# Experts' last biases gathered per slot, and a table of token ids in place of an array of dispatched rows

## The chip, the cores and the metric

The kernel runs on one core of a Trainium2 chip. The metric is the device time of one execution in microseconds (us). The engines are named as in the profile: PE (TensorE, the matmuls), PEld (PE's weight loads), DVE (VectorE), ACT (ScalarE), POOL (GpSimd) and SP (SyncE, which here issues most DMAs).

## The reference, cut to what matters

Two transformer layers run over x of 8 x 256 x 512, that is 2048 tokens of width C = 512, all in fp32. In the first layer attention and a mixture of experts read the same normalized tokens, and both results are added to x. The change touches the last biases of that mixture, b3 and sb3 below, and the way in which tokens get to their experts.

```python
xn = layernorm(x)
x  = x + lightning_attention(xn) + experts(xn)   # 32 heads of 128, decays, silu, RMS norm, gate
# experts: 16 of width 128, each token goes to 2 of them with a gate
for e in range(16):
    h = silu(xn @ w1[e] + b1[e]) * (xn @ w2[e] + b2[e])
    y = y + gate[:, e, None] * (h @ w3[e] + b3[e])
z = silu(xn @ sw1 + sb1) * (xn @ sw2 + sb2) @ sw3 + sb3   # shared expert of width 256, every token
experts = y + z
xn = layernorm(x)
x  = x + attention(xn) + low_rank_experts(xn)    # second layer
```

## The kernel before

The tokens stand in NCH = 4 chunks of CH = 512, each of TPC = 4 tiles of P = 128 tokens. The work is laid out in four stages.

**The opening** (until 164 us of the profiled execution) goes over the chunks. For each, `begin` normalizes on DVE; `turn_rows` (L243) turns the tokens on PE into xT, with copies by DVE; xns goes to DRAM as xnd; `token_sums` makes sums of the turned tokens on POOL and stores them (xc); `shared_up` (L312) runs the shared expert's first two products; `route` (L271 on PE, then a chain on DVE that ends in `first_two` and the gates `ge`) selects the two experts of each token; `decays` makes attention's decay factors on ACT and stores them (dec); `clear` has SP write zeros to a quarter of xd. Then `share` handles the chunk before: `shared_down` turns the gates (L333), copies them (ACT, L335), multiplies them by the 17 rows of last biases (16 experts' and the shared one, tile `b3_t`, L338), adds the shared expert's last products into the same PSUM bank (L340), and DVE adds the bank to x. The sum is stored as xr (L349). So the gate-weighted sum of the experts' last biases is made here, by a matmul over 17 rows with a column of ones for the shared bias.

After the last chunk DVE works out the slots (L475 to L523). Each expert's tokens are padded to whole tiles of 128, which makes NMT = 47 tiles and NSLOT = 6016 slots. `slots` has the slot of each token and choice, `slot_gates` its gate, `rows_` the rows of the expert's weights for each tile.

**The first pass of attention** (to 760 us; pass i = 0, on chunk 0) has NG = 8 units of 4 heads (g = 0 to 7). Products are made in seven parts p1 to p7 (`product`, L666), from sums of token blocks and sums of weights; the latter are made here by DVE and POOL and stored (ws) for the passes to come. Beside it `row` loads tiles of xnd (L1089), and `scatter` (L1094) writes their rows by an indirect DMA of POOL into xd, the array of dispatched rows, 2 x 16 times.

**Passes 1 to 3** (to 2510 us) have 24 units of some 75 us. Into them the 47 expert tiles are spread. A planner, `later(n, f)`, puts a piece of work n of its steps ahead, and `slot()` takes the pieces that are due. One `Expert` is four pieces: the start loads its rows xe from xd (SP, L696) and gathers its weights by `rows_` (POOL, L697), both into one buffer of `staged` (2 buffers, also used for weight blocks and for x); `turn`, 8 steps later, transposes the rows on PE; `up`, after 11, has the two products and their gating (L716); `down`, after 14, has the last product (L728), a copy by ACT to `ye` (L733) and the store to yd. `gather` and `settle` at the end of the passes read yd back by token, and multiply by the gates. At the end of each pass `load_sum` (L937) loads the chunk's xr on SP, and `finish` (L592) adds attention's sums to it on DVE; the result is stored as xs_. For the last chunk `next_x` (L1295) does the same in the tail.

**The tail** (to 2854 us) is the second layer. Its low-rank experts' products stand at L1434 and L1512.

The planner's order is kept as written on ACT and POOL (`manual_schedule`); on DVE, PE and SP the scheduler orders the instructions. Most tiles are rotated by name: tag "sum" has 3 buffers (ye, the loaded rows, others), `cp` 5. The helper `tt` at L97 issues all element-wise operations of two operands, so that many groups of the profile have that line; their tiles tell them apart. `Parts` cuts one large tile (`disp`, tag "acc", which attention later uses for its accumulators) into small ones, and `work` is the pool of the opening, whose memory attention takes over when it closes.

Of the kernel before, what the change touches and what calls it, by code (L numbers as in the profile page):

```python
# [18 lines left out]
P = 128  # L19
# [47 lines left out]
def block_kernel(  # L67
# [74 lines left out]

    def once(shape, name):
        return work.tile(shape, FP, tag=name, name=name, bufs=1)
# [19 lines left out]
    nc.sync.dma_start(out=bsh_t, in_=b_sh)  # L164
    b3_t = held[0 : E + 1, SH * C : (SH + 1) * C]
    nc.sync.dma_start(out=b3_t, in_=b3)
    for i in range(1, NCH):
# [6 lines left out]
    dram = ctx.enter_context(tc.tile_pool(name="dram", bufs=1, space=bass.MemoryType.DRAM))  # L174
    xd = dram.tile([NSLOT, C], FP, name="xd")
    yd = dram.tile([NSLOT, C], FP, name="yd")
# [5 lines left out]
    ]  # L182
    xnd = [dram.tile([P, TPC, C], FP, name=f"xnd{i}") for i in range(NCH)]
    dec = [dram.tile([P, 2, S + P], FP, name=f"dec{n}") for n in range(H // 2)]
# [3 lines left out]
    xr = [dram.tile([P, TPC, C], FP, name=f"xr{i}") for i in range(NCH)]  # L188
    zero = held[:, (SH + 1) * C : (SH + 2) * C].unsqueeze(1)
    nc.gpsimd.memset(zero, 0.0)  # L190

# [8 lines left out]

    before = once([P, E, E], "before")
    nc.gpsimd.memset(before, 1.0)
# [6 lines left out]

    dist = const.tile([P, S + P], FP, name="dist")  # L210
    nc.gpsimd.iota(
# [53 lines left out]
    def route(xT, ge, sel):  # L265

        full = [P, TPC, E]
        pl = ps_sc()
        for t in range(TPC):
            for c in range(NC):  # L270
                mm(  # L271
                    pl[:, bass.ts(t, E)], xT[:, c, bass.ts(t, P)], rw[:, c, :],
                    start=(c == 0), stop=(c == NC - 1),
                )
# [31 lines left out]
        tt(ge[:, :, 0:E], sc, sel, ALU.mult)  # L306
        nc.vector.memset(ge[:, :, E : E + 1], 1.0)

# [20 lines left out]
    def shared_down(i, hT):  # L329
        xc = xs[i]  # L330
        pg = ps_sc()
        for t in range(TPC):
            nc.tensor.transpose(pg[0 : E + 1, bass.ts(t, P)], gates[i][:, t, :], ident)  # L333
        gT = work.tile([E + 1, CH], FP, tag="geT", name="geT", bufs=1)
        nc.scalar.copy(gT, pg[0 : E + 1, :])  # L335
        for t in range(TPC):
            py = ps_mm()
            mm(py, gT[:, bass.ts(t, P)], b3_t, start=True, stop=False)  # L338
            for e in range(SH):
                mm(py, hT[:, e, bass.ts(t, P)], w3sh[:, e, :], start=False, stop=(e == SH - 1))  # L340
            tt(xc[:, t, :], py, xc[:, t, :], ALU.add)


    xT, gates, xns = [], [], []
    sel_all = once([P, NTT, E], "sel_all")

    def share(i, hT):
        shared_down(i, hT)
        nc.sync.dma_start(out=xr[i], in_=xs[i])  # L349

# [58 lines left out]

    def clear(i):  # L410
        lo, hi = (0, 12, 24, 36, NMT)[i : i + 2]
        nc.sync.dma_start(
            out=xd[lo * P : hi * P, :].rearrange("(j p) c -> p j c", p=P),
            in_=zero.to_broadcast([P, hi - lo, C]),
        )

    def begin(i):
# [5 lines left out]
    for i in range(NCH):  # L423
        xT.append(work.tile([P, NC, CH], FP, tag="xT", name=f"xT{i}", bufs=3))
        for t in range(TPC):
            turn_rows(xT[i], xns[i], t, ps_mm())
        nc.sync.dma_start(out=xnd[i], in_=xns[i])
        if i + 1 < NCH:
# [7 lines left out]
        ups.append(shared_up(i))  # L436
        ge = once([P, TPC, E + 1], f"ge{i}")
        route(xT[i], ge, sel_all[:, bass.ts(i, TPC), :])
        gates.append(ge)
        decays(i)  # L440
        clear(i)
        if i > 0:
# [6 lines left out]
    rows_ = const.tile([P, NMT], I32, name="rows_")  # L449
    disp = Parts(accp.tile([P, 7 * CH], FP, tag="acc", name="disp"))  # L450

# [48 lines left out]
    own = disp.tile([P, NMT], FP, name="own")  # L500
    nc.vector.tensor_reduce(own, owner, AX.X, ALU.add)
    nc.vector.tensor_scalar(own, own, float(E - 1), float(P), ALU.min, ALU.mult)
    nc.vector.tensor_scalar(rows_, own, part, None, ALU.add)
# [13 lines left out]
    for n in range(TOP):  # L517
        tt(hit, slot, ends_[:, n, :].unsqueeze(2).to_broadcast(full), ALU.is_equal)
        tt(hit, hit, sel_all, ALU.mult)
        for i in range(NCH):  # L520
            at_i = bass.ts(i, TPC)
            tt(hit[:, at_i, :], hit[:, at_i, :], gates[i][:, :, 0:E], ALU.mult)
        nc.vector.tensor_reduce(slot_gates[:, n, :], hit, AX.X, ALU.add)  # L523
# [62 lines left out]
    def finish(i, r):  # L586

        for b in range(2):
            for t in range(2):
# [3 lines left out]
                    o, acc[i][:, 2 * b : 2 * b + 2, t], all_rms[i][:, n : n + 1], o, ALU.mult, ALU.add  # L593
                )

    def spare8():
        return staged("spare")[:, 0 : TPC * C].rearrange("p (t c) -> p t c", t=TPC)

    with tc.tile_pool(name="attn", bufs=1) as attn, tc.manual_schedule(engines={mybir.EngineType.Activation, mybir.EngineType.Pool}):
# [79 lines left out]
        def slot():  # L679
# [3 lines left out]
            while pieces and pieces[0][0] <= now[0] and n < (2 if len(pieces) > 12 else 1):  # L683
                f = pieces.pop(0)[2]
                f()
                n += getattr(f, "func", f).__name__ not in ("silu", "gate", "row", "scatter", "load_sum", "sums1", "sums2", "sums3", "sums4", "settle0", "settle1", "out_sum")


        class Expert:


            def __init__(self, j):
                self.j = j
                xw = staged("xw")
                self.xe, self.we = xw[:, 0:C], xw[:, C:]
                nc.sync.dma_start(out=self.xe, in_=xd[bass.ts(j, P), :])  # L696
                nc.gpsimd.indirect_dma_start(  # L697
# [5 lines left out]
            def turn(self):  # L703
# [3 lines left out]
                self.xeT = attn.tile([P, NC, P], FP, tag="cp", name="xeT", bufs=5)  # L707
                nc.vector.tensor_copy(self.xeT, pt.rearrange("p (c n) -> p c n", c=NC))

            def up(self):  # L710
# [15 lines left out]
            def down(self):  # L726
# [5 lines left out]
                ye = attn.tile([P, C], FP, tag="sum", name="ye", bufs=3)  # L732
                nc.scalar.copy(ye, py)  # L733
                nc.sync.dma_start(out=yd[bass.ts(self.j, P), :], in_=ye)
# [75 lines left out]
        class Unit:  # L810
# [122 lines left out]
            def load_sum(self):  # L933

                if self.i + 1 < NCH:
                    self.r = spare8()
                    nc.sync.dma_start(out=self.r, in_=xr[self.i])  # L937

            def done(self):
# [140 lines left out]
        def expert(j):  # L1080
            e = Expert(j)
            later(8, e.turn)
            later(11, e.up)
            later(14, e.down)

        def row(t):

            x_ = attn.tile([P, C], FP, tag="sum", name="row", bufs=3)
            nc.sync.dma_start(out=x_, in_=xnd[t // TPC][:, t % TPC, :])  # L1089
            for n in range(TOP):  # L1090
                later(6 + 10 * n, partial(scatter, x_, t, n))

        def scatter(x_, t, n):
            nc.gpsimd.indirect_dma_start(  # L1094
                out=xd[:, :],
                out_offset=bass.IndirectOffsetOnAxis(ap=slots[:, n, t : t + 1], axis=0),
                in_=x_, in_offset=None, bounds_check=NSLOT - 1, oob_is_err=False,
            )

# [77 lines left out]
        for n, (i, g, p) in enumerate(plan):  # L1177
# [6 lines left out]
            if k == 0:  # L1184
# [104 lines left out]
    def next_x(i):  # L1289
# [332 lines left out]
```

## Time and profile before

| What | Value |
|---|---|
| runs before | 2852.0, 2856.99 and 2861.1 us, median 2856.99 |
| profiled execution | 2856.16 us, its span 2854.4 us |
| mean granted clock of TensorE | 0.993 |
| instructions | 49572 |
| moved in the span | 596 MB read from HBM, 163 MB written, 266 GB/s |

The durations below come from the one profiled execution. Its span is what the trace covers, and 1.8 us of its own time lie around that. In rows of the timeline stand start, length, engine, line, operation, output and inputs, shapes, type and count; the bracket gives the idle time of the engine ahead of the row, and what ended it. In rows of groups stand count, then busy time and mean ns of one, then the idle time ahead and its causes. In rows of DMA issues stand the queue, the kind, the count, and the median us from issue to landing.

### The profile page before, as it was taken

How to read it: one execution, taken by the hardware profiler on the slowest of the kernel's cores; microseconds unless marked ns; L12 is line 12 of the kernel's file. 1: busy time of each engine (PE TensorE's matmuls, PEld its weight loads, DVE VectorE, ACT ScalarE, POOL GpSimd, SP SyncE). 2: the span in 40 equal slices, each digit the busy share in tenths (PEclk: the TensorE clock that was granted, in tenths of full speed). 3: DMA queues.
4: the chain of work that ended last, by engine and by line, in shares of the span. 5: the costliest groups of instructions: out<-in, count | busy, mean ns of one | idle time of the engine just before them, and what ended most of it. 6: DMA issues, size and time to landing. Idle time of an engine off the chain costs nothing. (4 is left out here: it accounts for less than half of the span.)

```text
span 2854.4 us, 49572 instructions
## 1 busy us (share of the span) xinstructions
PE 2796.7 (98%) x19864; PEld 2566.1 (90%) x19864; DVE 1569.7 (55%) x2615; ACT 948.2 (33%) x1683; POOL 1465.7 (51%) x1213
## 2 busy tenths in 40 slices
PE   8989999999999999999999999999999999999999
PEld 4469999999999999999999999999999999987877
DVE  6555666666654445444545555555555555556663
ACT  3312222212244333333443333443444333432221
POOL 4545666665546555555645454545544566552210
PEclk9999999999999999999999999999999999999999
DMA  7888998899986777778877777777777788652211
GB/s 255 301 309 337 357 352 341 341 349 347 364 320 246 262 266 273 282 270 299 296 265 257 264 266 265 259 274 280 284 259 259 267 310 298 222 212 88 76 61 61
DMA packets 161943, 763.21 MB, mean 267 GB/s; under 512 B 18209, under 2 KB 24225, under 8 KB 109874
## 3 DMA queue, kind: packets, MB, share of 16 engines
q1 hardware_dynamic: 149826, 706.25, 66.9%
q0 software_dynamic: 11888, 53.79, 5.2%
q8 instruction: 157, 2.57, 0.4%
q14 instruction: 72, 0.59, 0.1%
HBM read 596.14 MB, written 163.05 MB: 266 GB/s over the span
## 5 line engine op out<-in xcount | busy, mean ns | idle before, releaser
L666 PE MATMUL ps_a<-xt,w 128*128 128x128 f32 x5376 | 750.9, 276 | 11.7 <-DVE r L97 7.7
L666 PEld LDWEIGHTS ps_a<-xt,w 128*128 128x128 f32 x5376 | 681.9, 192 | 30.1 <-issue 14.3
L97 POOL TENSOR_TENSOR c<-c 128x512 f32<-128x512 f32 x216 | 271.7, 1273 | 262.0 <-DVE c L97 259.9
L97 POOL TENSOR_TENSOR c<-c,r 128x512 f32<-128x512 f32 x240 | 318.4, 1347 | 158.9 <-DVE r L97 153.1
L666 PE MATMUL ps_e<-xt,w 128*128 128x128 f32 x2688 | 373.4, 275 | 1.3 <-DVE c L97 1.3
L97 POOL TENSOR_TENSOR sums<-sums,sq 128x512 f32<-128x512 f32 x120 | 153.3, 1278 | 426.4 <-ACT sq L796 425.6
L996 ACT COPY cp<-ps_a 128x512 f32<-128x512 f32 x336 | 196.4, 585 | 476.0 <-PE ps_a L666 468.8
L666 PEld LDWEIGHTS ps_e<-xt,w 128*128 128x128 f32 x2688 | 344.4, 192 | 11.2 <-issue 3.8
L97 POOL TENSOR_TENSOR w<-w 128x512 f32<-128x512 f32 x224 | 294.6, 1325 | 108.2 <-issue 31.2
L666 PE MATMUL ps_a<-w,xt 128*128 128x128 f32 x1792 | 346.7, 275 | 0.0
L858 PE MATMUL ps_sc<-wo,gT 128*128 128x256 f32 x1288 | 305.1, 379 | 1.8 <-POOL gT L97 1.8
L97 DVE TENSOR_TENSOR acc<-ps_sc,acc 128x512 f32<-128x512 f32 x208 | 143.3, 690 | 265.8 <-PE ps_sc L858 198.8
L666 PEld LDWEIGHTS ps_a<-w,xt 128*128 128x128 f32 x1792 | 272.3, 192 | 0.0
L97 DVE TENSOR_TENSOR c<-ps_a,c 128x512 f32<-128x512 f32 x232 | 157.9, 686 | 202.7 <-PE ps_a L666 201.7
L858 PEld LDWEIGHTS ps_sc<-wo,gT 128*128 128x128 f32 x1288 | 232.3, 190 | 26.8 <-POOL gT L97 2.0
L666 PE MATMUL ps_b<-xt,w 128*128 128x128 f32 x1680 | 236.4, 277 | 6.8 <-ACT c L1010 4.2
L801 DVE SCALAR_TENSOR_TENSOR gT<-ps_o,nw,c 128x256 f32<-128x256 f32 x256 | 112.0, 479 | 231.0 <-ACT sq L796 222.0
L666 PEld LDWEIGHTS ps_b<-xt,w 128*128 128x128 f32 x1680 | 217.3, 194 | 17.5 <-issue 8.2
L744 ACT ACTIVATE c<-c 128x512 f32<-128x512 f32 x256 | 148.9, 627 | 170.1 <-DVE c L97 170.0
L796 ACT ACTIVATE sq<-ps_o 128x512 f32<-128x512 f32 x120 | 71.6, 597 | 382.3 <-PE ps_o L782 382.3
L666 PE MATMUL ps_e<-w,xt 128*128 128x128 f32 x896 | 173.2, 275 | 0.0
L97 DVE TENSOR_TENSOR s<-ps_sc,decay 128x384 f32<-128x384 f32 x256 | 139.8, 552 | 40.7 <-PE ps_sc L770 38.1
(299 smaller groups left out, 4635.8 us busy)
## 6 DMA issues: line engine op xcount, KB each, us to landing
w<-in_w_att_dram SPq DMA_DIRECT2D x128, 1024.0 KB
st<-in_w_att_dram SPq DMA_DIRECT2D x32, 1024.0 KB
wo<-in_w_out_dram SPq DMA_DIRECT2D x113, 256.0 KB
decay<-dec SPq DMA_DIRECT2D x64, 384.0 KB
w<-ws0p SPq DMA_DIRECT2D x12, 1792.0 KB
w<-ws1p SPq DMA_DIRECT2D x12, 1792.0 KB
w<-ws2p SPq DMA_DIRECT2D x12, 1792.0 KB
w<-ws3p SPq DMA_DIRECT2D x12, 1792.0 KB
```

Source lines behind the costliest of these rows:

```text
L97: (eng or nc.vector).tensor_tensor(o, a, b, op)
L666: mm(bank[:, bass.ts(ty, P)], a, b, start=(first and ty == 0), stop=True, skip_group_check=True,)
L744: nc.scalar.activation(qk, qk, AF.Silu)
L796: nc.scalar.activation(sq, po, AF.Square)
L801: nc.vector.scalar_tensor_tensor(gT[:, h, :].rearrange("p (t n) -> p t n", t=2), po[:, bass.ts(h, S)].rearrange("p (t n) -> p t n", t=2), ...
L858: mm(py[:, bass.ts(t, S)], self.O[p][:, hh, bass.ts(t, P)], self.wo[p][:, hh, :], start=(t == 0 and hh == 0), stop=(hh == 1), skip_group_c ...
L996: nc.scalar.copy(c, bank)
```

## The change

The gate-weighted bias matmuls of the opening go away. Each expert tile gathers its last bias once per slot: a DMA of POOL reads row `own_[j]` of b3 into all 128 rows of xe, after the rows of tokens in xe have been turned, and DVE adds it as it moves the last product out of PSUM. The shared expert's last bias is loaded as a row to 128 partitions, and POOL adds it to xr where attention's sums are added (`last_bias`).

The array xd, its clears, the row loads and the scatters of rows go away too. A `table` in DRAM, one int32 per slot, is zeroed once; token ids are scattered into it in the first pass of attention (32 indirect DMAs of POOL, 4 bytes a row). The last unit of that pass reads the table and turns it (`whose`), and each expert gathers its rows from xnd by it, on POOL's queue instead of SP's. An empty slot has token 0. Besides, `before`, `sel_all`, `ge` and the slot arithmetic share the tile `disp`, `dist` is in the opening's pool, the stores of xr keep the order of the program, and the steps of an expert's pieces are 10, 12, 13 and 18 instead of 8, 11 and 14.

```diff
+    disp = Parts(accp.tile([P, 7 * CH], FP, tag="acc", name="disp"))
...
-    b3_t = held[0 : E + 1, SH * C : (SH + 1) * C]
-    nc.sync.dma_start(out=b3_t, in_=b3)
...
-    xd = dram.tile([NSLOT, C], FP, name="xd")
+    table = dram.tile([NSLOT, 1], I32, name="table")
...
-    zero = held[:, (SH + 1) * C : (SH + 2) * C].unsqueeze(1)
-    nc.gpsimd.memset(zero, 0.0)
+    none = once([NMT, P], "none", I32)
+    nc.gpsimd.memset(none, 0)
+    nc.sync.dma_start(out=table.rearrange("(j p) o -> j (p o)", p=P), in_=none)
...
-    before = once([P, E, E], "before")
+    before = disp.tile([P, E, E], FP, name="before")
...
-    dist = const.tile([P, S + P], FP, name="dist")
+    dist = once([P, S + P], "dist")
...
     def shared_down(i, hT):
         xc = xs[i]
-        pg = ps_sc()
-        for t in range(TPC):
-            nc.tensor.transpose(pg[0 : E + 1, bass.ts(t, P)], gates[i][:, t, :], ident)
-        gT = work.tile([E + 1, CH], FP, tag="geT", name="geT", bufs=1)
-        nc.scalar.copy(gT, pg[0 : E + 1, :])
         for t in range(TPC):
             py = ps_mm()
-            mm(py, gT[:, bass.ts(t, P)], b3_t, start=True, stop=False)
             for e in range(SH):
-                mm(py, hT[:, e, bass.ts(t, P)], w3sh[:, e, :], start=False, stop=(e == SH - 1))
+                mm(py, hT[:, e, bass.ts(t, P)], w3sh[:, e, :], start=(e == 0), stop=(e == SH - 1))
             tt(xc[:, t, :], py, xc[:, t, :], ALU.add)
...
-    sel_all = once([P, NTT, E], "sel_all")
+    sel_all = disp.tile([P, NTT, E], FP, name="sel_all")
 
     def share(i, hT):
         shared_down(i, hT)
-        nc.sync.dma_start(out=xr[i], in_=xs[i])
+        tc.keep_in_program_order(nc.sync.dma_start(out=xr[i], in_=xs[i]))
...
-        ge = once([P, TPC, E + 1], f"ge{i}")
+        ge = disp.tile([P, TPC, E], FP, name=f"ge{i}")
...
-        clear(i)
...
+    token = const.tile([P, NTT], I32, name="token")
+    nc.gpsimd.iota(token, pattern=[[P, NTT]], base=0, channel_multiplier=1)
...
+    def last_bias(r, t3):
+        nc.sync.dma_start(out=t3, in_=b3[E : E + 1].to_broadcast([P, C]))
+        for t in range(TPC):
+            add(r[:, t, :], r[:, t, :], t3, nc.gpsimd)
...
                 xw = staged("xw")
                 self.xe, self.we = xw[:, 0:C], xw[:, C:]
-                nc.sync.dma_start(out=self.xe, in_=xd[bass.ts(j, P), :])
+                nc.gpsimd.indirect_dma_start(
+                    out=self.xe, out_offset=None, in_=xnd[:, :],
+                    in_offset=bass.IndirectOffsetOnAxis(ap=whose[:, j : j + 1], axis=0),
+                    bounds_check=NT - 1, oob_is_err=False,
+                )
...
+            def bias(self):
+                nc.gpsimd.indirect_dma_start(
+                    out=self.xe, out_offset=None, in_=b3[:, :],
+                    in_offset=bass.IndirectOffsetOnAxis(ap=own_[:, self.j : self.j + 1], axis=0),
+                    bounds_check=E, oob_is_err=False,
+                )
...
                 ye = attn.tile([P, C], FP, tag="sum", name="ye", bufs=3)
-                nc.scalar.copy(ye, py)
+                add(ye, py, self.xe)
...
                     nc.sync.dma_start(out=self.r, in_=xr[self.i])
+                    last_bias(self.r, attn.tile([P, C], FP, tag="sum", name="sb3", bufs=3))
...
-            later(8, e.turn)
-            later(11, e.up)
-            later(14, e.down)
-
-        def row(t):
-            x_ = attn.tile([P, C], FP, tag="sum", name="row", bufs=3)
-            nc.sync.dma_start(out=x_, in_=xnd[t // TPC][:, t % TPC, :])
-            for n in range(TOP):
-                later(6 + 10 * n, partial(scatter, x_, t, n))
-
-        def scatter(x_, t, n):
+            later(10, e.turn)
+            later(12, e.bias)
+            later(13, e.up)
+            later(18, e.down)
+
+        def scatter(t, n):
             nc.gpsimd.indirect_dma_start(
-                out=xd[:, :],
+                out=table[:, :],
                 out_offset=bass.IndirectOffsetOnAxis(ap=slots[:, n, t : t + 1], axis=0),
-                in_=x_, in_offset=None, bounds_check=NSLOT - 1, oob_is_err=False,
+                in_=token[:, t : t + 1], in_offset=None, bounds_check=NSLOT - 1, oob_is_err=False,
             )
+
+        def read_table():
+            rows = attn.tile([P, P], I32, tag="h1", name="rows")
+            nc.sync.dma_start(out=rows[0:NMT], in_=table.rearrange("(j p) o -> j (p o)", p=P))
+            byno = attn.tile([P, P], FP, tag="he", name="byno")
+            def turn_table():
+                nc.vector.tensor_copy(byno[0:NMT], rows[0:NMT])
+                pt = ps_sc()
+                nc.tensor.transpose(pt[:, 0:NMT], byno[0:NMT, :], ident[0:NMT, 0:NMT])
+                nc.vector.tensor_copy(whose, pt[:, 0:NMT])
+            later(16, turn_table)
...
                 if i == 0:
-                    for e in range(2):
-                        later(1 + 24 * e, partial(row, 2 * g + e))
+                    for e in range(5 * g, min(5 * g + 5, TOP * NTT)):
+                        later(5 + 10 * (e - 5 * g), partial(scatter, e // TOP, e % TOP))
+                    if g == NG - 1:
+                        later(4, read_table)
...
             nc.sync.dma_start(out=x_, in_=xr[i])
+            last_bias(x_, work.tile([P, C], FP, tag="sb3", name="sb3", bufs=1))
             finish(i, x_)
```

More of the change, by code (lines that the diff above doesn't have):

```diff
@@ L141, in block_kernel, with once @@
     work = opening.enter_context(tc.tile_pool(name="work1", bufs=2))
-    def once(shape, name):
-        return work.tile(shape, FP, tag=name, name=name, bufs=1)
+    def once(shape, name, dtype=FP):
+        return work.tile(shape, dtype, tag=name, name=name, bufs=1)
+    disp = Parts(accp.tile([P, 7 * CH], FP, tag="acc", name="disp"))
     scratch = big("scratch").rearrange("p (h b) n -> p h (b n)", h=4)
@@ L182, in block_kernel @@
     ]
-    xnd = [dram.tile([P, TPC, C], FP, name=f"xnd{i}") for i in range(NCH)]
+    xnd = dram.tile([NT, C], FP, name="xnd")
     dec = [dram.tile([P, 2, S + P], FP, name=f"dec{n}") for n in range(H // 2)]
@@ L305, in route @@
         first_two(sel, masked, E)
-        tt(ge[:, :, 0:E], sc, sel, ALU.mult)
-        nc.vector.memset(ge[:, :, E : E + 1], 1.0)
+        tt(ge, sc, sel, ALU.mult)
     def project(pm, wi, block, i):
@@ L408, in token_sums @@
             nc.sync.dma_start(out=xc[i][:, ORDER.index(p), 4:8], in_=t)
[L410 to L415, printed above, removed]
     def begin(i):
@@ L426, in block_kernel @@
             turn_rows(xT[i], xns[i], t, ps_mm())
-        nc.sync.dma_start(out=xnd[i], in_=xns[i])
+        nc.sync.dma_start(
+            out=xnd[i * CH : (i + 1) * CH, :].rearrange("(t p) c -> p t c", p=P), in_=xns[i]
+        )
         if i + 1 < NCH:
@@ L449, in block_kernel @@
     rows_ = const.tile([P, NMT], I32, name="rows_")
-    disp = Parts(accp.tile([P, 7 * CH], FP, tag="acc", name="disp"))
+    own_ = const.tile([P, NMT], I32, name="own_")
+    whose = const.tile([P, NMT], I32, name="whose")
+    token = const.tile([P, NTT], I32, name="token")
+    nc.gpsimd.iota(token, pattern=[[P, NTT]], base=0, channel_multiplier=1)
     earlier = disp.tile([P, P], FP, name="earlier")
@@ L501, in block_kernel @@
     nc.vector.tensor_reduce(own, owner, AX.X, ALU.add)
+    nc.vector.tensor_scalar(own_, own, float(E - 1), None, ALU.min)
     nc.vector.tensor_scalar(own, own, float(E - 1), float(P), ALU.min, ALU.mult)
@@ L521, in block_kernel @@
             at_i = bass.ts(i, TPC)
-            tt(hit[:, at_i, :], hit[:, at_i, :], gates[i][:, :, 0:E], ALU.mult)
+            tt(hit[:, at_i, :], hit[:, at_i, :], gates[i], ALU.mult)
         nc.vector.tensor_reduce(slot_gates[:, n, :], hit, AX.X, ALU.add)
@@ L685, in slot @@
                 f()
-                n += getattr(f, "func", f).__name__ not in ("silu", "gate", "row", "scatter", "load_sum", "sums1", "sums2", "sums3", "sums4", "settle0", "settle1", "out_sum")
+                n += getattr(f, "func", f).__name__ not in ("silu", "bias", "gate", "read_table", "scatter", "load_sum", "sums1", "sums2", "sums3", "sums4", "settle0", "settle1", "out_sum")
         class Expert:
@@ L708, in turn @@
                 nc.vector.tensor_copy(self.xeT, pt.rearrange("p (c n) -> p c n", c=NC))
+            def bias(self):
[3 more added lines that the diff above has]
+                    bounds_check=E, oob_is_err=False,
+                )
             def up(self):
```

## The prediction

> **What bounds the kernel.** I read the page's first part, then the windows cut at the stages, then TensorE's (PE's) timeline of the opening, then what other engines and DMA queues show wherever the change touches them. In the windows the columns are: stretch, its length, busy time of PE, of its weight loads, of VectorE (DVE), ScalarE (ACT) and GpSimd (POOL), granted clock, DMA share, GB/s.
>
> ```profile
> PE 2796.7 (98%) x19864; PEld 2566.1 (90%) x19864; DVE 1569.7 (55%) x2615; ACT 948.2 (33%) x1683; POOL 1465.7 (51%) x1213
> ```
> ```profile
> 0.00:58.50 58.50, 47.29 (x152) 29.10 (x153) 40.21 (x88) 22.81 (x31) 27.98 (x45) 0.94 0.74 267
> 58.50:164.40 105.90, 96.93 (x288) 44.50 (x286) 56.11 (x113) 30.28 (x48) 53.96 (x84) 0.94 0.76 285
> 164.40:200.00 35.60, 27.39 (x217) 26.51 (x216) 24.02 (x55) 6.84 (x11) 7.24 (x6) 0.95 0.85 313
> 200.00:760.00 560.00, 555.34 (x4296) 535.92 (x4295) 347.04 (x533) 121.75 (x210) 343.81 (x269) 1.00 0.91 347
> 760.00:2240.00 1480.00, 1472.69 (x11235) 1400.70 (x11234) 744.48 (x1136) 584.83 (x1049) 781.79 (x616) 1.00 0.75 274
> ```
>
> PE is the bound from 200 us on: it idles 4.7 us in the first pass of attention (200 to 760) and 7.3 us in the 1480 us in which the experts run. There, work taken from DVE, ACT, POOL or the DMA queues can win at most those few us; work added to them can lose much more, if it makes PE wait. Only matmuls removed, and waits removed in the opening, buy time.
>
> **The opening, what goes.** Four times, once a chunk, the old code turns the gates (L333), copies them (ACT, L335) and adds bias products (L338) ahead of the shared expert's own products (L340). The last two chunks on PE (start, length, what; in brackets the idle time before):
>
> ```profile
> 131.91 1.12 PE L338 MATMUL ps_b<-held,geT 17*128 17x512 f32 x2 [0.67 <-ACT geT L335]
> 132.96 1.98 PE L340 MATMUL ps_b<-held,scratch 128*128 128x512 f32 x4
> ...
> 147.41 0.61 PE L333 MATMUL ps_sc<-ident,ge 128*17 128x128 f32 x4 [3.58 <-DVE ge L97]
> ...
> 149.58 2.07 PE L338 MATMUL ps_b<-held,geT 17*128 17x512 f32 x2
> 151.58 3.78 PE L340 MATMUL ps_b<-held,scratch 128*128 128x512 f32 x4
> 155.29 1.27 PE L338 MATMUL ps_a<-held,geT 17*128 17x512 f32 x2
> ```
>
> One bias product takes 1.05 us from start to start (131.91 to 132.96). Twelve at 1.05 are 12.6 us; the last chunk's four are 2.00, 1.20, 1.05 and 1.05, so 5.3. The turn and the wait for its copy take 1.26 us in each of three chunks (130.65 to 131.91), 3.8. In the last chunk the turn (0.45) waits 3.58 for the router's gates; afterwards PE runs slow, and L340 takes 3.71 instead of 1.92 (1.8). In all 12.6 + 5.3 + 3.8 + 0.45 + 3.58 + 1.8 = 27.5 us.
>
> **What of it is given back.** After the shared expert PE turns the next chunk, and that needs PSUM banks and the copies (xT) that DVE makes among its routing work:
>
> ```profile
> 75.16 0.66 PE L243 MATMUL ps_a<-ident,xn 128*128 128x128 f32 x4 [1.32 <-DVE x L97]
> 76.97 3.48 PE L271 MATMUL ps_sc<-rw,xT 128*128 128x16 f32 x16 [1.15 <-DVE xT L248]
> ```
>
> PE would come 5.5 us earlier (4 x 1.05 + 1.26) to this point, but DVE is solid here from 63.7 to 76.8. It gains only what leaves its chain: the ACT copy of 0.57 ahead of the exponential, and, at the first boundary, four normalizations of 0.54 which the built program's order now has earlier, with the gaps they cause. I take its xT copy 3.4 us earlier at the first boundary and 2.6 at the second; 2.1 and 2.9 are given back, 5.0. The second boundary had no slow clock; with some 3 us of idle it will: at the first one 1.32 + 1.15 us of idle made the next matmuls 3.48 instead of 1.96 and 5.50 instead of 3.60, together 3.4 us. So 27.5 - 5.0 - 3.4 = 19 us. The Trainium skill, "TensorE: Matmul & The Clock Gate", section "What's actually happening", has the clock fall only after an idle window of about 3.4 us; by it the second boundary would cost nothing and the time would be 3.4 us lower. The row at 76.97 slowed after less, so I go by the row.
>
> In the last chunk the shared products no longer wait for the router, so both remaining groups run back to back and attention starts while DVE still routes. Its second product then waits for ACT, as now:
>
> ```profile
> 175.33 0.58 ACT L1010 COPY c<-ps_b 128x512 f32<-128x512 f32 x1 [26.64 <-DVE disp L97]
> ```
>
> This copy writes memory of the opening, and waits for the opening's last users: so far DVE's slot arithmetic, afterwards the stores of x. In the built order the slot arithmetic's tiles have left that memory; the last store is issued about 17 us after the last router matmul, and x<-xr, as large, lands in 5.4. So PE idles here about as now (4.20) and I count nothing. If the stores came much later, some 11 of the 19 us would be held here; 8 to 27.5 are the ends.
>
> **First pass of attention.** 12.3 MB of clears (3 x 3072 + 2816 KB), 16 row loads and 32 scatters of 256 KB leave the DMA engines; DMA is at 0.91 here, but PE idles 4.7 us only: counted at nothing, at most 4.7 gained. POOL issues 32 scatters as before (about 1.0 us each). They move 4 bytes a row. No row shows so small a transfer; it can lie anywhere from below the 7.3 us of the 2 KB rows to several times that. In the built order the last scatter stands in the unit before the one that reads the table, tens of us earlier, and that hides it either way. "DMA: Bandwidth & Descriptors", "Specifications", says that transfers under 512 B are read, modified and written; the same cover would hide it.
>
> **The experts.** Here are the issue groups (count, and us from issue to landing) and the weight gather on POOL:
>
> ```profile
> xw<-in_w_exp_dram,rows__1106 POOLq DMA_INDIRECT x47, 7.5
> xd<-row,slots POOLq DMA_INDIRECT x32, 7.3
> spare<-yd,slots POOLq DMA_INDIRECT x32, 6.2
> ```
> ```profile
> L697 POOL DMA_INDIRECT xw<-in_w_exp_dram,rows__1106 x47 | 47.5, 1011 | 6.8 <-DVE acc L97 0.6 <-issue 0.5 <-PE ps_o L782 0.2
> L733 ACT COPY ye<-ps_sc 128x512 f32<-128x512 f32 x47 | 27.5, 585 | 75.2 <-PE ps_sc L728 64.0 <-POOL wo L97 11.2
> ```
>
> POOL gets 2 x 47 more gathers of 1.01, 95 us, into 698 us of idle; DVE gets 47 additions of about 0.69 (its rows that read PSUM), 32 us, into 735; ACT loses 27.5. Behind POOL's gathers queue its additions into c, sums and gT, for which ACT and PE wait; behind DVE's addition queue the evictions that free PE's banks. With POOL or DVE late each time, 47 x 0.69 = 32 us could come through; nothing if the idle takes all. PE waits for POOL once now (1.8 us), so I go near the lower end: 2.5 us. A gain is excluded, since PE's own expert work stays.
>
> **The shared bias, added by POOL.** Three times four additions of 1.27 (5.1 us) come into POOL's queue at the end of a pass. The built order has them long after their 1 MB load in the second and third pass, but close behind the load of the bias row. POOL may stand for one landing (5.4) each time; 0 to 3 x 10.5 = 31 us, hidden by POOL's idle half. I take 2. The fourth is in the tail, where DVE's next step is already late:
>
> ```profile
> 2728.32 2.74 DVE L592 SCALAR_TENSOR_TENSOR x<-acc,rms,x 128x512 f32<-128x512 f32 x4 [1.91 <-DMA x<-xr]
> ```
> ```profile
> 2732.84 1.99 PE L1434 MATMUL ps_e<-t,fa 128*128 128x256 f32 x8 [1.85 <-DVE cp L97]
> ```
>
> POOL's four additions (4 x 1.3) start when x lands, 2728.3; the last of L592 (0.74) ends at 2734.3 instead of 2731.06. The eviction behind it is what PE waits for already: 3.3 us, all on the path. Ends: 0, and 5.2 if nothing overlaps.
>
> **Sum.** Against the profiled execution's own 2856.16 (span 2854.4 and 1.8 around it): -19.1 + 2.5 + 2 + 3.3 = -11.3, so 2845. The median of the runs, 2857.0, is 0.8 above that execution; I leave the forecast at 2845.
>
> **Rivals.**
> *The bias rows land late* (slower). DVE's addition of ye now waits for a gather which POOL may only issue once PE has turned the rows. In the built order 7.8 to 13.3 us of PE work (0.2235 a matmul of 128 columns, from this timeline) lie between the gather's place and the down product; with that product, 9.0 at the least, in about 20 of the 47 experts. POOL lags its place by 0.6 to 3.4 us (the old weight gather started 6.6 to 12.7 us ahead of the turn, while its place says 9.8 to 14.1). With the 6.2 us of the 2 KB gathers: in time. With 3.4 + 7.5 = 10.9, 1.9 us late, DVE stands, and PE behind it: 20 x 1.9 = 38 us, 2883. It decides from 1 us late (20 us eat the gain and 0.3% more). For it: every expert reads one row 128 times, which no row shows. Against: the median of 6.2. The same skill page, "Anatomy of one DMA", would give 2.6 us for 256 KB as an estimate, and no such rival; the trace's 6.2 stands.
> *The opening gives little* (no change): the stores of x or the loads behind them hold attention's start, 8 us are won and 7.8 lost: 2856. For it: the idle at 175 shows that release is already late. Against: those stores are issued earlier in the built order.
> *The opening gives all* (27.5, and POOL's and DVE's new work hides): only the tail's 3.3 is lost, 2832.
>
> **Chances.** Forecast 0.52, opening gives all 0.14 (both faster), opening gives little 0.16 (the same), late bias 0.18 (slower). 0.3%, about 9 us, is what these measurements can tell from no change. The range goes from 2832 to 2870, which takes in the third rival, the second, and the first up to two thirds of a us late.
>
> **What would show it.** Right: no L338 or L333; attention's first products about 18 us earlier; PE's busy time about 18 us lower; the tail's wait ahead of L1434 grown by some 3 us; idle of PE between 760 and 2240 below 12 us. Wrong: DVE waiting for a DMA ahead of ye in many experts; POOL waiting for the bias row; ACT's first copy of c still near 175.

## The result, and the profile after

The changed kernel takes 2989.5 us (2982.9 to 2995.7, four runs) against 2856.9: 1.046 times as long, 95% interval 1.043 to 1.050. The forecast was 2845. The profiled execution has a span of 2981.2 us. Of the runs below, e1, e3, e4, f2 and h1 were timed once each, the others four to ten times.

The first fence is the page's first part, the second the same windows as before.

```profile
PE 2814.0 (94%) x19817; PEld 2593.2 (87%) x19817; DVE 1600.0 (54%) x2661; ACT 920.5 (31%) x1631; POOL 1573.4 (53%) x1324
```
```profile
0.00:58.50 58.50, 47.68 (x156) 29.38 (x157) 41.08 (x84) 27.78 (x39) 29.23 (x47) 0.94 0.70 246
58.50:164.40 105.90, 94.38 (x384) 58.53 (x384) 70.03 (x158) 25.04 (x41) 51.06 (x85) 0.89 0.71 263
164.40:200.00 35.60, 31.39 (x243) 30.48 (x242) 18.89 (x33) 6.66 (x12) 19.99 (x17) 0.95 0.93 224
200.00:760.00 560.00, 462.93 (x3303) 440.04 (x3301) 251.86 (x405) 96.10 (x166) 265.93 (x213) 0.90 0.90 253
760.00:2240.00 1480.00, 1457.12 (x11116) 1387.27 (x11117) 793.23 (x1196) 541.88 (x967) 883.21 (x712) 1.00 0.78 284
```

Read the row from 200 to 760. PE was busy for 555 of the 560 us, now for 463, and runs at a granted clock of 0.90 instead of 1.00 (which is also why its busy time in all is higher, with fewer matmuls). The DMA engines are as busy as before (0.90 against 0.91), but move 253 GB/s instead of 347. They are not idle and not loaded with more bytes: what they do takes longer. The packet records of the traces show it too: of the packets of 8 KB that start in this stretch, 322 take over 2 us each (the longest 8.7), before the change 2.

The opening gained what was forecast: attention's first product starts at 144.18 (164.38 before), and its second at 153.32 (175.97).

```profile
144.18 0.83 PE L664 MATMUL ps_b<-xt,w 128*128 128x128 f32 x6
...
153.32 0.94 PE L664 MATMUL ps_b<-xt,w 128*128 128x128 f32 x6 [0.57 <-ACT c L1021]
```

What PE waits for, summed over the span (total us, times, longest), is headed by operands of attention and by weights from DRAM:

```profile
PE ps_sc L888 <- DVE gT L811: 47.6, 10, 9.0
PE ps_sc L779 <- DVE acc L97: 23.5, 3, 9.4
PE ps_b L664 <- DMA w<-in_w_att_dram: 20.1, 3, 13.6
```

To see where the time went, here are seven marks of each profiled execution, as us later (+) or earlier than in the one before: PE's first product of attention; DVE's 17th, 49th, 57th, 145th and 249th of 256 instructions that make gT (eight a unit; these begin the third, seventh and last unit of the first pass, the unit behind those with three experts, and the last unit of attention); and the span's end. The absolute times before are 164.4, 360.0, 662.9, 735.0, 1568.3, 2507.5 and 2854.4.

| Run | product | 17th | 49th | 57th | 145th | 249th | end | time, us |
|---|---|---|---|---|---|---|---|---|
| the change | -20.2 | +24.3 | +106.3 | +112.0 | +124.3 | +125.1 | +126.8 | 2989.5 |
| e1_before_plus_ids | +1.0 | +31.9 | +97.6 | +107.6 | +121.2 | +120.6 | +119.8 | 2975.9 |
| x1_before_plus_spread | +8.5 | +8.5 | +9.3 | +8.6 | +8.2 | +8.5 | +8.7 | 2861.3 |
| e2_rows_again | -29.5 | -10.3 | -11.0 | -11.8 | +4.8 | +3.0 | +7.0 | 2860.7 |
| e3_ids_512_bytes | -23.7 | -33.7 | -20.1 | +20.9 | +37.4 | +37.0 | +39.7 | 2895.8 |
| e4_ids_apart | -22.0 | -32.0 | -24.9 | +14.8 | +31.3 | +32.7 | +36.9 | 2893.1 |
| f1_ids_64_apart | -16.1 | -26.0 | -17.0 | +1.8 | +18.0 | +17.6 | +21.6 | 2876.6 |
| f2_ids_spread_24kb | -25.0 | -34.7 | -29.8 | -21.3 | -8.0 | -8.5 | -2.3 | 2853.8 |
| g1_steps_earlier | -16.5 | -26.4 | -16.7 | +0.4 | +35.3 | +39.4 | +43.6 | 2900.4 |
| h1_no_last_bias | -18.2 | -28.1 | -21.1 | -1.4 | +14.5 | +17.4 | +17.9 | 2874.1 |
| v1_up_later | -20.5 | -30.2 | -29.6 | -21.3 | -19.0 | -18.3 | -20.9 | 2833.9 |
| v2_rows_by_act | -25.1 | -34.8 | -32.7 | -26.8 | -24.5 | -23.8 | -24.5 | 2833.9 |
| v3_steps_9_12 | -25.0 | -34.7 | -33.5 | -25.6 | -16.1 | -16.0 | -17.5 | 2844.4 |

Row one: 20 us won in the opening, 132 lost between the first product and the 57th gT, 12 in the units with three experts, some 2 in the tail.

In the lossy stretch the scatters stand in POOL's timeline, and the DMA view of the same 40 us has one figure for each us (busy tenths, then GB/s):

```profile
318.91 0.99 POOL L1100 DMA_INDIRECT table<-token,slots  x1 [0.16 <-issue]
...
339.12 1.00 POOL L1100 DMA_INDIRECT table<-token,slots  x1 [0.15 <-issue]
```
```profile
DMA  5689999999399098667649999999999999996465
GB/s 57 262 369 502 414 418 430 391 428 399 140 131 33 0 66 33 25 41 49 82 98 451 451 385 378 451 471 405 393 451 459 401 401 427 352 98 25 16 33 49
```

A scatter is issued at 318.91; from 320 to 331 the rate falls from about 400 GB/s to 140 and less, mostly under 100, while the engines still count as busy for some six tenths of the time. At 331 it is back at 451. The next scatter, at 339.12, is followed by the same hole from 345 on. This is what the following experiments took apart.

### The profile page after: what moved, and what is told of

Its sections match the earlier page's. It is cut to its first block, busy times and chain, and to the rows that moved or that the text cites. A ratio compares the mean times of both kernels' runs of the same rounds, so it can differ in the third digit from the quotient of the medians.

```text
span 2981.2 us, 49621 instructions
## 1 busy us (share of the span) xinstructions
PE 2814.0 (94%) x19817; PEld 2593.2 (87%) x19817; DVE 1600.0 (54%) x2661; ACT 920.5 (31%) x1631; POOL 1573.4 (53%) x1324
## 4 chain that ended last, share of the span: by engine, by line
PE 72%; DMA 13%; DVE 8%; issue 3%; POOL 3%; ACT 0%; SPq 0%; DVEq 0%; POOLq 0%; ACTq 0%
PE ps_a L664 20%; PE ps_e L664 11%; PE ps_sc L868 9%; DMA w<-in_w_att_dram 6%; PE ps_b L664 5%; PE ps_o L791 3%; PE ps_sc L779 3%; PE ps_sc L726 3%; PE ps_sc L888 2%; DMA st<-in_w_att_dram 2%; PE ps_a L1535 2%; PE ps_o L792 2%; PE ps_sc L780 2%; DVE w L97 1%; PE ps_sc L738 1%
## 5 line engine op out<-in xcount | busy, mean ns | idle before, releaser
L664 PEld LDWEIGHTS ps_a<-xt,w 128*128 128x128 f32 x5376 | 690.0, 194 | 35.5 <-issue 17.5
L664 PE MATMUL ps_e<-xt,w 128*128 128x128 f32 x2688 | 380.1, 278 | 13.4 <-DVE c L97 12.8
L868 PE MATMUL ps_sc<-wo,gT 128*128 128x256 f32 x1288 | 304.8, 379 | 1.8 <-POOL gT L97 1.8
L664 PE MATMUL ps_b<-xt,w 128*128 128x128 f32 x1680 | 238.3, 279 | 25.0 <-DMA w<-in_w_att_dram 20.1
L664 PEld LDWEIGHTS ps_b<-xt,w 128*128 128x128 f32 x1680 | 216.1, 195 | 33.7 <-issue 30.2
L888 PE MATMUL ps_sc<-wo,gT 128*128 128x256 f32 x576 | 149.6, 407 | 47.6 <-DVE gT L811 47.6
L97 DVE TENSOR_TENSOR w<-w,st 128x512 f32<-128x512 f32 x128 | 89.3, 734 | 175.6 <-DMA w<-in_w_att_dram 122.7
```

Of the source, the lines that this page charges most:

```text
L97: (eng or nc.vector).tensor_tensor(o, a, b, op)
L664: mm(bank[:, bass.ts(ty, P)], a, b, start=(first and ty == 0), stop=True, skip_group_check=True,)
L868: mm(py[:, bass.ts(t, S)], self.O[p][:, hh, bass.ts(t, P)], self.wo[p][:, hh, :], start=(t == 0 and hh == 0), stop=(hh == 1), skip_group_c ...
L888: mm(py[:, bass.ts(h, S)], gT[:, hh, bass.ts(t, P)], self.wo[pair, h][:, hh, :], start=(h == 0 and hh == 0), stop=(hh == 1), skip_group_ch ...
```

## The experiments

**1. Is it the scatter of ids?** To the kernel before, behind each scatter of rows, a scatter of 4-byte values is added:

```diff
+            nc.gpsimd.indirect_dma_start(out=table[:, :],
+                out_offset=bass.IndirectOffsetOnAxis(ap=slots[:, n, t : t + 1], axis=0),
+                in_=rows_[:, t : t + 1], in_offset=None, ...)
```

> The kernel before, and behind each of its 32 scatters of rows one more scatter of 128 values of 4 bytes, into a table that nothing reads. Theory A (each scatter of 4-byte values holds up all other DMA traffic for some 10 us, so that weights and their sums come late to PE): the first pass of attention grows by some 130 us, 2985 us, with less than 290 GB/s from 200 to 760 us. Theory B (the loss comes from POOL's order or from other edits, not from the transfers): POOL is busy for 32 x 1.0 us more, half of it hidden, 2857 to 2875 us, and the rate stays near 347 GB/s.

Measured: 2975.9 us, 118.6 above the runs of before, and 286 GB/s from 200 to 760 us, where 385 packets of 8 KB take over 2 us. Theory A holds: the added transfers alone, with nothing else of the change, cost nearly all that the change lost (132.6).

**2. Does the loss go when rows are dispatched again?**

```diff
-                nc.gpsimd.indirect_dma_start(out=self.xe, ..., in_=xnd[:, :], ... whose ...)
+                nc.sync.dma_start(out=self.xe, in_=xd[bass.ts(j, P), :])
... (row, scatter of rows, clear and xd as in the kernel before; no table)
```

> The changed kernel, but rows are dispatched as before (array xd, its clears, row loads and scatters of 2 KB rows; experts load xe from xd); all bias edits, the moved tiles and the later steps of the experts stay. Theory A: the loss of the first pass goes; what is left is the opening's gain of 20 us, 13 us lost in the units with three experts and 2 in the tail: 2850 us (2840 to 2860). Theory B: the other edits carry the loss, and it stays above 2950 us.

Measured: 2860.7 us, ratio 1.0008 (0.9997 to 1.0020). The loss of the first pass is gone, as theory A has it; the sum was 10 us too low. Attention's first product leads by 29.5 us here, but only 10 of them are kept at the 17th gT. This is the second rival of the prediction, seen here and not in the change. PE's second product, ACT's first copy, and SP's last store of x in this run:

```profile
165.40 1.65 PE L668 MATMUL ps_b<-xt,w 128*128 128x128 f32 x6 [21.87 <-ACT c L1021]
```
```profile
164.76 0.59 ACT L1021 COPY c<-ps_b 128x512 f32<-128x512 f32 x1 [41.68 <-DMA xr<-x]
```
```profile
159.33 0.38 SPq L342 DMA_DIRECT2D xr<-x  x1
```

The copy waits for the store of x, which SP issues at 159.33, right behind the last store of the token sums; in the change the last such store is issued at 146.33. The sums are late because POOL waited 47.1 us for earlier stores of sums to land (11.8 in the change). In the opening the edits of the two runs differ in the clears alone, apart from the zeroing of the 24 KB table and the token numbers. So, from one execution of each, part of the opening's gain hangs on the clears having gone.

**3. Size, or place?** Two variants of the table: 512 bytes written to each slot, and 4 bytes written to slots that lie 512 bytes apart.

```diff
# e3: rows of 128 ids
-                in_=token[:, t : t + 1], ...
+                in_=wide[t], ...                       # [P, 128], all the token's id
# e4: 4 bytes, slot s at word 128 * s
-                out_offset=bass.IndirectOffsetOnAxis(ap=slots[:, n, t : t + 1], axis=0),
+                out_offset=bass.IndirectOffsetOnAxis(ap=apart[:, n, t : t + 1], axis=0),
```

> The changed kernel, but each slot has 512 bytes in the table, and each scatter writes 128 rows of 512 bytes, all of them the token's id; the number of scatters and of rows is the same. Theory A in the form that the small size is what costs: 2850 to 2865 us. If the number of scattered rows costs, or POOL's order (theory B): 2975 us or more.

> The changed kernel with slots 512 bytes apart in the table, but 4 bytes written to each, as in the change. Theory A by size: as slow as the change, 2985 us. Theory C (it is not the size, but that 6016 neighbours share 24 KB of DRAM and their writes meet at one place): 2850 to 2870 us.

Measured: 2895.8 and 2893.1 us. Up to the 49th gT both are 20 to 25 us ahead of before, so neither the count of rows nor the size of 4 bytes costs much; the place does (theory C). The expected totals were missed for a cause of the variants' own: they lose 40 us in one unit, where SP reads the table back in words 512 bytes apart. In the second variant that read and SP's next issue, and the DMA view from 670 to 720 (busy tenths, then GB/s, each figure 1.25 us):

```profile
672.41 0.84 SPq L1114 DMA_DIRECT2D rows<-table  x1
673.31 37.32 SPq L928 DMA_DIRECT2D wo<-in_w_out_dram  x1
```
```profile
DMA  9979310000000000000000000000000009999999
GB/s 434 374 308 406 131 7 1 1 1 1 1 1 1 1 1 1 1 1 1 1 1 1 1 1 1 1 1 1 1 1 1 1 1 256 252 339 365 341 387 411
```

For some 33 us the 6016 reads of 4 bytes are nearly all that moves, at 1 GB/s. The DMA engines are not full of them: they count as idle. What stands is SP, which issues most DMAs: its next issue lasts 37.32 us, and until then it issues no other load.

**4. A crowded region, or neighbouring words?**

```diff
# f1: slot s at word 16 * s (385 KB), read back in rows of 8 KB
+    nc.vector.tensor_scalar(apart, ends_, 16.0, None, ALU.mult)
# f2: slot 128 j + p at word 47 p + j (24 KB as in the change), read back as [128, 47]
+    tt(apart, ends_, tile_of, ALU.add)     # 47 * slot + j * (1 - 6016)
```

> The changed kernel with the table's slots 64 bytes apart, 4 bytes written to each, and the table read back in 47 rows of 8 KB into SBUF, of which DVE takes every 16th word (in the run with slots 512 bytes apart, reading single words of 4 bytes cost some 40 us). Theory C1 (writes of neighbouring words of the same few bytes meet each other): the scatters cost nothing at 64 bytes either: 2848 to 2856 us. Theory C2 (it is the small region of 24 KB; 385 KB are less crowded, but not as little as 3 MB): between, 2870 to 2950 us.

> The changed kernel with the table of 24 KB as it is, 4 bytes written to each slot, but slot 128 j + p at word 47 p + j, so that neighbouring slots of a tile lie 188 bytes apart; it is read back straight into the layout that the experts use, without the turn. Theory C1 (neighbouring words): 2848 to 2860 us. Theory C2 (the small region): as slow as the change, 2975 us or more.

Measured: 2876.6 us (ratio 1.0059, 1.0040 to 1.0078) and 2853.8. The second run decides: same region, same size, same count, and between the 17th and the 49th gT it loses 4.9 us where the change loses 82. It is the neighbouring words (theory C1): here 2 packets of 8 KB take over 2 us between 200 and 760. The run with 64 bytes between slots lies between the two expected times, but not through its scatters: 9 us in that same stretch. It starts attention 9 us later than the other run and loses 19 us at the unit in which the table is read, against 8.5. Why its opening is later was not tried.

**5. The same in the kernel before.** Experiment 1 with the words spread as in the run that decided:

```diff
-                out_offset=bass.IndirectOffsetOnAxis(ap=slots[:, n, t : t + 1], axis=0),
+                out_offset=bass.IndirectOffsetOnAxis(ap=apart[:, n * NTT + t : n * NTT + t + 1], axis=0),
```

> The kernel before with 32 more scatters of 128 values of 4 bytes, as in the first run of this study, but slot 128 j + p goes to word 47 p + j of the 24 KB table; same count, size, place in POOL's order and region. Theory C1 (neighbouring words of one DMA meet): 2857 to 2870 us, POOL's issues being all that is left, and more than 335 GB/s from 200 to 760 us. If it is the count, the size or the region: 2970 us, as in that run.

Measured: 2861.3 us, ratio 1.000 (0.998 to 1.002), where neighbouring words cost 118.6 us. The rate from 200 to 760 is 346 GB/s, and no packet of 8 KB takes over 2 us there. (The profiled execution had an opening 8.5 us longer, at a clock of 0.87; the marks behind it stay at that distance.) A scatter and the rates around it, in the same 40 us as for the change:

```profile
320.67 0.97 POOL L1111 DMA_INDIRECT table<-rows__1107,apart  x1 [0.30 <-issue]
```
```profile
GB/s 408 410 385 303 438 414 332 459 301 74 375 442 352 279 352 385 188 131 410 328 180 301 453 442 434 426 410 426 426 242 422 426 442 401 434 397 422 434 381 399
```

No hole of 10 us follows the scatter at 320.67; the lowest single figure behind it is 131.

**6. The 13 to 17 us in the passes with experts.** One row of PE in a unit with three experts, in the change, and DVE ahead of it:

```profile
1098.02 2.05 PE L726 MATMUL ps_sc<-xeT,xw 128*128 128x128 f32 x16 [1.28 <-DVE xeT L710]
```
```profile
1093.90 3.47 DVE L97 TENSOR_TENSOR c<-c,r 128x512 f32<-128x512 f32 x2
1097.29 0.68 DVE L710 COPY xeT<-ps_sc 128x512 f32<-128x512 f32 x1
```

PE has turned the rows at 1093.2; DVE first does two additions of 1.73 us and copies them at 1097.29; PE wants them at 1096.7 (1098.02 less the 1.28 of waiting). Two variants of the 64-byte run tell the steps from the new work:

```diff
# g1
-            later(10, e.turn)
-            later(12, e.bias)
-            later(13, e.up)
-            later(18, e.down)
+            later(8, e.turn)
+            later(10, e.bias)
+            later(11, e.up)
+            later(16, e.down)
# h1
-            later(12, e.bias)
-                add(ye, py, self.xe)
+                nc.scalar.copy(ye, py)
-            last_bias(x_, work.tile([P, C], FP, tag="sb3", name="sb3", bufs=1))
```

> As the run with slots 64 bytes apart, and the pieces of an expert two steps earlier: 8, 10, 11 and 16 instead of 10, 12, 13 and 18. Theory S (the turn at step 10 falls where DVE has four copies and sums queued, so the copy of the turned rows comes 1.3 us late in every unit with three experts): the waits of PE for xeT go and the time is 9 to 13 us under that of the other run. Theory N (POOL's gathers and DVE's additions are too much wherever they stand): within 3 us of the other run.

> As the run with slots 64 bytes apart, with steps 10, 13 and 18, but the experts' last biases are left out (no gather, ACT copies ye again), and the shared bias of the last chunk is left out of the tail. Theory S: PE's waits for xeT of 1.3 us in the units with three experts stay, and with them the 13 us of the expert passes. Theory N: they go, and the passes take as long as before the change. In the tail PE's wait ahead of the low-rank products falls back from 3.5 to some 1.9 us, and the tail is 2 to 4 us shorter.

Measured: 2900.4 us (1.015, 1.013 to 1.018) and 2874.1. Without any last bias the passes lose 15.9 us between the 57th and the 145th gT, with it 16.2, and the waits stay as they were. So POOL's 47 bias gathers and DVE's additions cost nothing there. Earlier steps are no cure, against what theory S had me expect. PE's waits in the change and, in the same words, in e2 (total us, times, longest), then in the run without biases, and in the run with earlier steps:

```profile
PE ps_sc L726 <- DVE xeT L710: 7.7, 6, 1.3
```
```profile
PE ps_sc L732 <- DVE xeT L716: 7.7, 6, 1.3
```
```profile
PE ps_sc L714 <- DMA xw<-xnd,whose: 13.2, 8, 2.6
```

With the turn at step 8 the gather of the rows, now on POOL's queue, has not landed (eight waits, 1.65 us in the mean), and the passes lose 34.9 us. In e2 the rows come from xd on SP's queue, so POOL has no gather of rows; with the later steps kept, it has the same six waits and loses 16.6 us. So the later steps pay for the gather, and the price of them, with or without it, is that the copy falls behind other work of DVE. In the tail, the run without the last chunk's shared bias loses 0.5 us from the 249th gT on; with it f1 loses 4.0.

**7. Versions that come out ahead.** All three take the spread table of f2, and add the last chunk's shared bias in the first pass, to the stored sums:

```diff
# all: in units 1 to 4 of the first pass, one tile of 128 tokens each
+            add(x_, x_, t3, nc.gpsimd)
+            nc.sync.dma_start(out=xs_[NCH - 1][:, t], in_=x_)
# v1
-            later(13, e.up)
+            later(14, e.up)
# v2
-                nc.vector.tensor_copy(self.xeT, pt.rearrange("p (c n) -> p c n", c=NC))
+                nc.scalar.copy(self.xeT, pt.rearrange("p (c n) -> p c n", c=NC))
# v3: steps 9, 11, 12 and 17
```

> The run with the table's neighbours spread (24 KB, slot 128 j + p at word 47 p + j), with two edits. The up product of an expert stands at step 14 instead of 13, so that DVE's late copy of the turned rows has landed: by theory S PE's six waits of 1.3 us go, and more where the same lateness shifts later units; the passes with experts lose 3 to 8 us instead of 16. The shared bias of the last chunk is added in the first pass of attention (tile by tile, stored beside the other chunks), not in the tail: the tail falls by 4 us. Together 2838 to 2845 us; if POOL's and DVE's new work were what costs (theory N), 2850 us.

> As the other run with the tail's bias moved, but step 13 for the up product as in the change, and ACT copies the turned rows to xeT in place of DVE (ACT no longer copies ye). By theory S the waits for xeT go here too: 2836 to 2845 us. If the wait comes from PE's or POOL's order and not from DVE's queue, they stay: 2850 us.

> As the other two, with steps 9, 11, 12 and 17, DVE's copy, and the tail's bias moved. At 8 the gather of rows by POOL landed up to 2.6 us after PE was there; at 10 DVE's copy was 1.3 us late. If both are simple distances, 9 loses about 1 us a unit on one or both: 2845 to 2855 us.

Measured: 2833.9 us (ratio 0.991, 0.988 to 0.994), 2833.9 (0.991, 0.989 to 0.994) and 2844.4 (0.995, 0.993 to 0.997). Both cures of the copy work: from the 57th to the 145th gT the first two lose 2.3 us where f2 lost 13.3 and the third loses 9.5. The tail, with its bias moved, takes 0.7 to 2.6 us less than before the change, in f2 it takes 6.2 more. Two different edits of the same wait give the same time, and both are faster than the kernel before, by 0.9%.

## Why the prediction was wrong, step by step

- **First pass of attention, counted at nothing: this step failed.** The prediction asked how late the table could be, found cover of tens of us, and said "that hides it either way". That much is so: nobody waited for the table. What it did not ask is what 32 small transfers do to the others on the same DMA engines, which stood at 0.91 busy. Measured: 126 us lost between the first product and the 49th gT, about 4 us of PE for each scatter (126 / 32). The writes to neighbouring words slow the other packets, and PE's operands come late. With the words spread (f2) the whole kernel takes 135.7 us less. "At most 4.7 gained" had no lower end below nothing, although the change put transfers there which no row of the trace showed.
- **The rule on small transfers.** The Trainium skill, "DMA: Bandwidth & Descriptors", section "Specifications", was cited for transfers under 512 B being read, modified and written. Read as a price of size, it does not fit these runs: 4 bytes and 512 bytes a row took the same time to 3 us (2893.1 and 2895.8, one run each), and 4 bytes in spread words cost nothing that can be measured (2861.3 against 2857.3).
- **Opening, 19.1 us: right in sum, partly by luck.** The first product starts 20.2 us earlier. But of the 2.6 us that the terms leave behind the second boundary (2 x 5.5 - 5.0 - 3.4), 0.3 were left. The second group of L312 there, before and in the change:

```profile
118.64 1.88 PE L312 MATMUL ps_a<-xT,wsh 128*128 128x512 f32 x4
```
```profile
118.36 1.88 PE L312 MATMUL ps_a<-xT,wsh 128*128 128x512 f32 x4
```

  At the first boundary PE idled 2.31 + 4.12 us in place of 1.32 + 1.15. The rest of the opening won 19.9 where the terms have 16.6; 1.7 of the difference are two products of the slot arithmetic (L482 and L483), which stood ahead of attention's start and now come behind it. Single executions scatter as well: with the opening of before, e1 and x1 start attention at +1.0 and +8.5, and v1 to v3, with one opening, at -20.5 to -25.1. Counting nothing for the wait at 175 was too careful: it shrank from 4.20 to 0.57, and in the runs without the holes attention's lead grew by another 10 us up to the 17th gT. In f2 the clock is 1.00 from 144 us on, where the kernel before had 0.95 from 164 to 200 and 0.96 from 200 to 240. The slow clock at the second boundary came, as expected from the row of before (granted clock 0.50 from 108.5 to 112.0), after 2.78 us of idle:

```profile
108.51 3.60 PE L272 MATMUL ps_sc<-rw,xT 128*128 128x16 f32 x16 [2.78 <-DVE xT L249]
111.94 6.58 PE L312 MATMUL ps_b<-xT,wsh 128*128 128x512 f32 x8
```

  Before, these took 1.96 and 3.68, so 4.5 us went here. The section "What's actually happening" of the Trainium skill's "TensorE: Matmul & The Clock Gate", by whose idle window of about 3.4 us nothing would have gone, does not agree with the 2.78 us taken alone. But the prediction's reading, that less idle time than that window slows PE, is not shown either. Right ahead of the idle time PE ran only turns (L244, L243 before). Without them, PE had no product for 5.0 us here (103.5 to 108.5) and for 4.4 us ahead of the row at 76.97 (72.5 to 77.0), and ran slow; at the second boundary of before it had none for 2.5 us (110.8 to 113.3), and the granted clock stayed at 1.00. If turns do not count as work, the window fits all three places; no run tried that.
- **The opening gives little.** This rival did not happen in the change, but something like it did in e2, where the clears came back (10 us kept of 29.5).
- **Experts, 2.5 us (0 to 32): in the range, wrong mechanism.** It was 12.3 in the change. Of the 95 us of gathers on POOL and 32 of additions on DVE, from which the step was made, the biases' half of the gathers and the additions cost nothing (h1), and without the rows' half the loss stays (e2, 16.6). The later steps cost it, and the rows' gather needs them (g1). This was not weighed: the text counted the gather's issue, not its distance to the turn. The sign of "idle of PE between 760 and 2240 below 12 us" failed: it is 22.9 in the change and 21.2 in f2.
- **Late bias rows.** DVE did wait for the bias gather, eight times and 14.5 us in all, but PE never behind it. So the rival's sign showed in 8 of 47 experts, and its loss did not.
- **Shared bias.** In the passes nothing shows of it: POOL waited once for the bias row (8.8 us), and PE nowhere behind it. In the tail PE's wait grew from 1.85 to 3.45, so by 1.6 and not by 3.3:

```profile
2853.27 5.74 DVE L584 SCALAR_TENSOR_TENSOR x<-acc,rms,x 128x512 f32<-128x512 f32 x4 [1.03 <-POOL x L97]
```
```profile
2860.27 1.99 PE L1457 MATMUL ps_e<-t,fa 128*128 128x256 f32 x8 [3.45 <-DVE cp L97]
```

  L584 takes 5.74 us with POOL's additions between its parts (2.74 before), as worked out. That execution's tail as a whole is 1.7 us longer, f1's and f2's 4.0 and 6.2.
- **PE's busy time 18 us lower: no.** It rose from 2796.7 to 2814.0: at a clock of 0.90 the matmuls from 200 to 760 took longer, 0.140 us of busy time each (462.93 / 3303) instead of 0.129.

Without the holes (f2) the change gives 2853.8 us in its one run, 5 below the runs of before beside it (2859.0), too little to tell from no change; with the distances of the experts and the tail mended, 2834. The step on the first pass was worth more than all the others together.

## What to carry to other kernels

A transfer that nobody waits for can still be the dearest one: where the DMA engines are nearly full and the bound engine lives on their next arrival, price a new transfer by what it does to the others, not only by its own landing. When single words are scattered, lay the table out so that values written by one DMA do not lie side by side, and read it back in runs of words, not word by word (in the unit of that read f2, with rows of 188 bytes, lost 8.5 us, the words 512 bytes apart 40). When a load moves to a later queue and its consumer is moved back to cover it, check where the consumer's own copy now falls in the next engine's queue.

## What the runs showed that was not expected

- 128 writes of 4 bytes, by one indirect DMA, to packed slots, of which those of one expert follow each other, took the traffic of all 16 DMA engines down from about 400 to mostly under 100 GB/s for some 10 us (the rates from 320 to 331). The same writes 188 bytes apart, in the same 24 KB, did not. What in the memory path does it is not in the trace; whether fewer neighbours, or other sizes side by side, do the same was not tried.
- One DMA of 6016 reads of 4 bytes, 512 bytes apart, kept the rate at 1 GB/s for some 33 us, with the DMA engines idle for most of it and SP held for 37.32 us in its next issue.
